# A two-layer block on one core: the mixing's weights multiplied first, and attention outputs with channels on the partitions

## The chip, the core and the metric

The kernel runs on one core of a Trainium2 chip. A core has five engines that run side by side, each with its own instruction queue that it works off in order: TensorE (PE, matrix products, results only into PSUM), VectorE (DVE), ScalarE (ACT, activation functions and scaled copies), GpSimd (POOL) and SyncE (SP), which here issues nearly all DMAs. PEld is the loading of TensorE's stationary operand. An engine waits for another through semaphores. The metric is the device time of one execution in microseconds (us), lower is better; times of several executions are given as a median.

## What is computed

The input `x` has 4 sequences of 256 tokens with 256 channels, in float32. Two layers follow, each with two residual steps: attention and a feed-forward part. Before each step, the activations are multiplied by a ratio that comes from a second input (a scan in both directions). All arithmetic is float32.

```python
x = x + L0_attn(L0_cond(x, ...), ...)     # gated delta rule, 32 value heads of 128 channels
x = x + L0_ffn(L0_cond2(x, ...), ...)     # 64 routed experts and a shared one
x = x + L1_attn(L1_cond(x, ...), ...)     # a gated mixing, see below
x = x + L1_ffn(L1_cond2(x, ...), ...)     # 8 routed experts
```

The change touches two of them. The end of the first layer's attention, where `core` are the attention outputs per head (128 channels, normalized by their own mean square), `z` are gates from the activations, and `norm_w` is a weight per channel:

```python
out = core * rsqrt(mean(core * core, -1) + EPS) * norm_w
out = out * silu(z)
return out @ w_out
```

And the second layer's mixing, with `W_in` of 1024 x 256 and `conv_w` of 512 x 512:

```python
xz = einsum('bsh,ih->bsi', hidden_states, W_in)
x, z = split(xz, 2, axis=-1)
x = einsum('bsk,ik->bsi', x, conv_w)
y = x * D
return einsum('bsi,hi->bsh', y * silu(z), W_out)
```

Nothing stands between the first half of `W_in` and `conv_w`, so the two products are one linear map of 256 channels onto 512.

## The kernel before

The 1024 tokens are worked in two halves `s` of 512 tokens (two sequences each). `x` stays in SBUF with channels on the partitions. Attention is worked in 32 units: 16 key heads by 2 halves. A unit holds one key head and its two value heads (`v`), two sequences (`b`) and two chunks of 128 tokens (`n`), so a tile of 128 x 512 holds all of one kind for a chunk. Four units form a group, for which small triangular inverses are computed together on VectorE; two units together are projected by `w_out` (`project`, L769) into one PSUM bank, and added to `x`.

In a unit, `products` (L882) makes keys, queries, norms and decay matrices; `values` (L1089) makes the values, turns them on TensorE to tokens on the partitions (`ps_vt`) and scales them on VectorE into `vo`; `outputs` (L1133) makes new values `vn0`, `vn1` and the outputs of the two chunks, `ps_at`, each copied by ScalarE into `vo`; `gates` (L1237) makes `z` with tokens on the partitions, and ScalarE's silu of it, `zs`; `normed` (L1301) makes the sums of squares with eight ScalarE activations with an accumulator (`junko`, `rs`), adds `eo` and takes the power −1/2 on GpSimd, multiplies by the roots and by `zs` on GpSimd, turns the result on TensorE (`ps_ot`, four transposes a bank) and evicts it through ScalarE, scaled by `norm_w`, into `oT` with channels on the partitions, which is what `project` needs.

After a half's attention follow `experts64` (L2013), `gated_mix` (L2114) and `experts8` (L2176). `gated_mix` makes four `xi` tiles and four `z` tiles of 128 x 512 by products that contract 256 channels (`ps_in`), then four mixing tiles that contract the 512 channels of `xi` (`ps_mix`), which VectorE multiplies by `D` and `z`, then `ps_out`.

**The order of the work** is set by a planner in the kernel, before it is built. Every step is recorded on a tape as an operation with an engine, an assumed cost, what it reads and writes, and how late its result lands (`Tape.op`, L195). `plan` (L292) places the operations one at a time: on each engine, among those that can start soon, the one whose latest allowed start is earliest. Numbers tuned for this kernel steer it: a price for a change of ScalarE's function table (`SWITCH`), for idle time (`IDLE`), for buffers taken early (`RATE`, `SPARE`), due times. `pushed` (L391) computes new latest starts from a plan; `run` (L405) repeats this `ROUNDS` times, here 10, and takes the shortest plan. The instructions are then issued in that order on each engine.

Tiles of 128 x 512 in SBUF share 59 places (`PLACES`); `MOST` (L1462) says how many each kind may hold. Six PSUM banks (`ps`) are shared in the same way. Two units of the first half (`EARLY`, heads 3 and 4) have their gates made early, in the opening, and kept in DRAM. Matmuls of float32 take two records each in the profile. All instructions are recorded through one helper, so that they have one line, L128 (L129 in the changed file); they are told apart by tile names.

Of the kernel before, what the change touches and what calls it, by code (L numbers as in the profile page):

```python
# [12 lines left out]
ALU = mybir.AluOpType  # L13
# [46 lines left out]
def _lay_out(i):  # L60
# [36 lines left out]
    d["winT"] = _rows(i["L1_attn_W_in"].T)  # L97
# [84 lines left out]
class Tape:  # L182
# [222 lines left out]
    def run(self):  # L405
# [7 lines left out]
        for o, (o.start, o.end, o.new) in zip(self.ops, min(plans)[2]):  # L413
            pass
# [6 lines left out]
ROUNDS, SWITCH, LOAD, SPARE, AHEAD, EACH, END, IDLE, MOMENT, GAP, RATE, GIVES = 10, 14.532, 1.3, 95.787, 163.973, 23.222, 1300.0, 54.829, 0.668, 62.664, 3.14, 4.877  # L421
UNIT = 42

EARLY, FEW = range(3, 5), 6
NORMS = 0.55
FOUR32, TWO64 = 0.75, 1.1
LAND = 3.0
WINDOW, ENOUGH, LITTLE, SLOW, THIN = 3.4, 0.471, 0.38, 0.5, 6.598
# [367 lines left out]
class Unit:  # L796
# [85 lines left out]
    def products(self):  # L882
# [107 lines left out]
        op("DVE", 0.78, shifted, [ps], [turned, k2, ki, self.eo])  # L990
# [98 lines left out]
    def values(self):  # L1089
# [17 lines left out]
        for n in range(2):  # L1107
# [13 lines left out]

            def scaled(n=n, ps=ps, vo=vo):
# [8 lines left out]
            op("DVE", _dve(512), scaled, [ps, self.kn], [vo])  # L1131

    def outputs(self):  # L1133
# [38 lines left out]
        def decayed():  # L1172
# [4 lines left out]
            "at0",  # L1177
            lambda q: self.attnT[0]()[:, q, :],
            lambda q: vn0()[:, q, :],
            [self.attnT[0], vn0],  # L1180
        )
        copied(lambda: vob(0), ps, vo[0])
        ps = product(
# [42 lines left out]
        ps = p.ps(f"at1_{self.tag}")  # L1226

        def second():
            for q in range(4):
                o = ps()[:, q * P : q * P + P]  # L1230
                e.tensor.matmul(o, qe()[:, q, :], vd()[:, q, :], start=True, stop=False)
                e.tensor.matmul(o, self.attnT[1]()[:, q, :], vn1()[:, q, :], start=False, stop=True)

        op("PE", 2 * cost, second, [qe, vd, self.attnT[1], vn1], [ps])
        copied(lambda: vob(1), ps, vo[1])

    def gates(self, early=False):  # L1237
# [4 lines left out]
        if self.kept:  # L1242
            for n, (kept, keptb) in enumerate(self.kept):
                zs = self.buf([P, 2, 2, P], "zs", 3, name=n)
# [11 lines left out]
        for n in range(2):  # L1256
            zs = self.buf([P, 2, 2, P], "zse" if early else "zs", 3, name=n)
            of.append(zs)
            ps = p.ps(f"z{n}_{self.tag}")

            def products(n=n, ps=ps):
                for b in range(2):
# [38 lines left out]
    def normed(self):  # L1301
# [8 lines left out]

        def o(n):
            return vo[n]().rearrange("p v b d -> p (v b) d")

        def roots(n):
            return rs()[:, n].rearrange("p v b -> p (v b)")

# [940 lines left out]
```

## Time and profile before

| | |
|---|---|
| time, median of 3 runs (lowest to highest) | 1409.51 us (1408.84 to 1413.2) |
| the profiled execution's own time | 1412.93 us |
| its span | 1411.1 us |
| its mean granted TensorE clock | 0.982 |
| ScalarE: table loads | 126, 161.7 us |
| ScalarE: squares `junko`, and reading the accumulator | 79.3 us and 47.8 us |
| ScalarE: `oT` from `ps_ot`, `vo` from `ps_at` | 40.4 us and 36.8 us |
| GpSimd: `vo` by the roots, `vo` by `zs`, the power | 66.8, 81.2 and 54.6 us |
| VectorE: `vo` from `ps_vt` | 42.1 us |
| VectorE: `turned` from `ps_kt` | 32 times, 14.2 us |
| DMA queue of SP | 35.5% of the 16 engines' time, 143.45 MB |

In the profile, a group line reads: line, engine, operation, out<-in by tile names, shapes, count | busy time, mean duration of one in ns | idle time of the engine just before these instructions and what ended it. Busy time is the union of the instructions' durations, and matmuls overlap, so busy time divided by the count is the spacing and the mean is the whole duration. A line of stages gives the stretch, its length, then the busy time of each engine with its number of instructions, the granted clock, the share of the DMA engines and their rate. A DMA line gives the tile, count, size and the median time from issue to landing.

### The profile page before, as it was taken

What the parts mean: (1) busy time and instruction counts of PE and PEld (TensorE: products, weight loads), DVE (VectorE), ACT (ScalarE), POOL (GpSimd) and SP (SyncE); (2) the same over time, 40 slices, a digit from 0 to 9 for tenths busy, and PEclk for the clock granted to TensorE, in tenths of its full rate; (3) what the DMA queues carried; (4) which work ended last, traced back from release to release, by engine and by line L of the source; (5) the groups of instructions that cost most, each with busy time, mean ns of one, the idle gap of its engine ahead of it and who ended that gap; (6) DMA issues with size and microseconds to landing.
All of it is one profiled execution on the core that took longest, in us unless ns stands there. A gap on an engine that the chain in (4) does not pass through costs nothing.

```text
span 1411.1 us, 24205 instructions
## 1 busy us (share of the span) xinstructions
PE 1321.2 (94%) x8428; PEld 817.4 (58%) x8428; DVE 1064.8 (75%) x2112; ACT 915.2 (65%) x1999; POOL 922.8 (65%) x913
## 2 busy tenths in 40 slices
PE   5986999999999899999999999999999999998988
PEld 3544766765875676766676576555455544443433
DVE  7889798787699588768769879867796787773123
ACT  1797799999889899988898898533434622211220
POOL 3189769979763988976885884487654666762032
PEclk9997999999999999999999999999999999999989
DMA  6412524412322353241351343544532324656030
GB/s 208 129 46 64 128 83 113 125 62 67 91 90 58 71 140 106 50 139 39 94 139 38 76 124 101 150 127 135 153 105 83 103 92 139 181 139 212 0 105 15
DMA packets 149817, 145.39 MB, mean 103 GB/s; under 512 B 76976, under 2 KB 93104, under 8 KB 149696
## 3 DMA queue, kind: packets, MB, share of 16 engines
q1 hardware_dynamic: 149264, 143.45, 35.5%
q8 instruction: 67, 1.10, 0.3%
q14 instruction: 54, 0.44, 0.1%
q10 hardware_dynamic: 432, 0.40, 0.1%
HBM read 129.75 MB, written 14.06 MB: 102 GB/s over the span
## 4 chain that ended last, share of the span: by engine, by line
PE 45%; DVE 25%; ACT 12%; POOL 7%; DMA 6%; issue 5%; SPq 1%; ACTq 0%; POOLq 0%; DVEq 0%
PE ps_h L128 5%; PE ps_a L128 4%; PE ps_ae L128 4%; PE ps_wo L128 4%; PE ps_e L128 4%; PE ps_z L128 4%; DVE xs L128 3%; DVE prod L128 3%; DVE accv_v L128 3%; PE ps_cvv L128 3%; PE ps_at L128 2%; DVE accq_q L128 2%; POOL attnT L128 2%; DMA w_w<-in_w 2%; ACT L128 2%
## 5 line engine op out<-in xcount | busy, mean ns | idle before, releaser
L128 ACT ACT_TABLE_LOAD x126 | 161.7, 1283 | 22.2 <-DVE sb_xT L128 10.4
L128 DVE SCALAR_TENSOR_TENSOR accv_v<-ps_cvv,sb_convw,accv_v 128x510 f32<-128x510 f32 (+2 forms) x192 | 141.8, 744 | 42.3 <-ACT accv_v L128 37.4
L128 PE MATMUL ps_z<-wz,ratio 128*128 128x256 f32 x480 | 118.7, 394 | 9.6 <-DVE vo L128 6.6
L128 POOL TENSOR_TENSOR hw_h<-hw_h,r_h 128x512 f32<-128x512 f32 x64 | 85.7, 1347 | 63.9 <-DVE hw_h L128 63.3
L128 PE MATMUL ps_h<-ratio,w_w 128*128 128x512 f32 x256 | 118.9, 598 | 6.6 <-DMA w_w<-in_w 5.7
L128 PE MATMUL ps_cvv<-ratio,wv 128*128 128x512 f32 x256 | 119.9, 601 | 2.9 <-ACT kqm L128 1.0
L128 ACT ACTIVATE r_h<-ps_h 128x512 f32<-128x512 f32 x64 | 38.2, 596 | 126.8 <-PE ps_h L128 126.5
L128 PE MATMUL ps_a<-hw_h,w_w 128*128 128x512 f32 x256 | 118.2, 593 | 0.0
L128 PE MATMUL ps_wo<-oT,wo 128*128 128x512 f32 x256 | 113.0, 593 | 0.0
L128 POOL TENSOR_TENSOR hw_e<-hw_e,r_e 128x512 f32<-128x512 f32 x32 | 41.6, 1322 | 101.0 <-DVE hw_e L128 101.0
L128 PEld LDWEIGHTS ps_z<-wz,ratio 128*128 128x128 f32 x480 | 90.1, 196 | 24.6 <-DVE vo L128 6.8
L128 PEld LDWEIGHTS ps_h<-ratio,w_w 128*128 128x128 f32 x256 | 47.0, 190 | 70.2 <-issue 55.1
L128 DVE TENSOR_TENSOR xs<-xs,prod 128x30 f32<-128x30 f32 (+14 forms) x240 | 81.2, 338 | 8.2
L128 DVE TENSOR_TENSOR prod<-xs,Rt 128x30 f32<-128x30 f32 (+14 forms) x240 | 78.5, 327 | 11.6 <-ACT xs L128 5.9
L128 ACT ACTIVATE junko<-vo 128x128 f32<-128x128 f32 x256 | 79.3, 310 | 7.6
L128 PE MATMUL ps_at<-vn,attnT 128*128 128x128 f32 x512 | 82.3, 277 | 1.5 <-ACT vn L128 1.4
L128 POOL TENSOR_TENSOR X<-attnT,kqm 128x512 f32<-128x512 f32 x64 | 82.8, 1313 | 1.2 <-ACT kqm L128 1.0
L128 POOL TENSOR_TENSOR vo<-vo,zs 128x512 f32<-128x512 f32 x64 | 81.2, 1288 | 1.6 <-ACT zs L128 1.6
L128 PEld LDWEIGHTS ps_wo<-oT,wo 128*128 128x128 f32 x256 | 48.1, 190 | 57.4 <-issue 52.6
L128 POOL TENSOR_TENSOR attnT<-attnT,sb_consts 128x512 f32<-128x512 f32 x56 | 70.7, 1280 | 15.5 <-DMA attnT<-G 8.5
L128 POOL TENSOR_TENSOR attnT<-attnT,kqm 128x512 f32<-128x512 f32 x64 | 80.6, 1278 | 0.1
L128 PEld LDWEIGHTS ps_a<-hw_h,w_w 128*128 128x128 f32 x256 | 47.9, 190 | 56.2 <-issue 52.6
(253 smaller groups left out, 3412.5 us busy)
## 6 DMA issues: line engine op xcount, KB each, us to landing
attnT<-G SPq DMA_DIRECT2D x64, 256.0 KB, 5.2
w_w<-in_w SPq DMA_DIRECT2D x64, 256.0 KB, 4.4
wb_wb<-w_rows SPq DMA_DIRECT2D x128, 128.0 KB, 3.6
wqk<-in_wqk SPq DMA_DIRECT2D x32, 256.0 KB, 4.2
wv<-in_wv SPq DMA_DIRECT2D x32, 256.0 KB, 4.2
wo<-in_wo SPq DMA_DIRECT2D x32, 256.0 KB, 3.8
qe<-G SPq DMA_DIRECT2D x32, 256.0 KB, 4.5
wz<-in_wz SPq DMA_DIRECT2D x30, 256.0 KB, 4.6
```

The source lines that it names most:

```text
L128: return self._tc.keep_in_program_order(f(*a, **k))
```

## The change

It has three parts and new numbers for the planner.

1. *The mixing's two weights are multiplied first* (`joined`, new). The first half of `W_in` and `conv_w` are loaded in six loads at the start, multiplied by eight matmuls of 512 columns into two tiles, copied by ScalarE and written to DRAM. `gated_mix` no longer makes `xi`; it loads the two product tiles and contracts the 256 channels of the activations with them.
2. *Attention outputs with channels on the partitions.* The operands of the output products are swapped, and `z` is made with its weight as the stationary operand (512 columns at once), so both come out with channels on the partitions and stay in PSUM or need no turning: no copy into `vo`, no `ps_ot`. The two chunks' outputs are made together, after both new values. ScalarE squares whole banks; TensorE sums the squares over the partitions with a matrix of ones (`ps_on`, eight matmuls, as for the keys); VectorE turns the sums and adds `eo`; GpSimd takes the power. The roots, with tokens on the partitions, are written to DRAM as rows (`rs`, 1024 values) and read back spread over all partitions (`rb`, two DMAs). VectorE multiplies the outputs by `norm_w` and `zs` into `oT`, and GpSimd multiplies `oT` by `rb`.
3. *The values are scaled by ScalarE*, in two halves, in place of one VectorE instruction.

The planner takes the last of 2 rounds' plans in place of the shortest of 10, has other prices, limits and due times, and a third unit's gates (head 5) are made early.

```diff
-        for o, (o.start, o.end, o.new) in zip(self.ops, min(plans)[2]):
+        for o, (o.start, o.end, o.new) in zip(self.ops, plans[-1][2]):
...
-ROUNDS, SWITCH, LOAD, SPARE, AHEAD, EACH, END, IDLE, MOMENT, GAP, RATE, GIVES = 10, 14.532, 1.3, 95.787, 163.973, 23.222, 1300.0, 54.829, 0.668, 62.664, 3.14, 4.877
-UNIT = 42
-EARLY, FEW = range(3, 5), 6
+ROUNDS, SWITCH, LOAD, SPARE, AHEAD, EACH, END, IDLE, MOMENT, GAP, RATE, GIVES = 2, 11.958, 1.3, 87.21, 174.585, 24.024, 1286.888, 56.776, 0.687, 66.3, 3.538, 5.035
+UNIT = 42.358
+EARLY, FEW = range(3, 6), 5
...
+            def evicted(n=n, ps=ps, vo=vo):
+                for b in range(2):
+                    e.scalar.activation(
+                        vo()[:, :, b, :],
+                        ps().rearrange("p (v b d) -> p v b d", v=2, b=2)[:, :, b, :],
+                        AF.Copy,
+                        scale=self.kn()[:, 2 * n + b : 2 * n + b + 1],
+                    )
...
-        copied(lambda: vob(0), ps, vo[0])
...
+        for v in range(2):
+            ps = p.ps(f"at{v}_{self.tag}")
+            self.out.append(ps)
+            def heads(v=v, ps=ps):
+                for b in range(2):
+                    q = 2 * v + b
+                    for n in range(2):
+                        o = ps()[:, (2 * b + n) * P : (2 * b + n) * P + P]
+                        last, vn = self.attnT[n]()[:, q, :], (vn0, vn1)[n]()[:, q, :]
+                        if n:
+                            e.tensor.matmul(o, vd()[:, q, :], qe()[:, q, :], start=True, stop=False)
+                        e.tensor.matmul(o, vn, last, start=not n, stop=True)
...
+                    e.tensor.matmul(ps(), wz()[:, k, v * P : v * P + P], p.act[s][:, k, :], start=k == 0, stop=k == 1)
...
+        op("PE", NORMS, norms, sqs, [sums], to=[turned, rs])
+        op("DVE", 0.66, shifted, [sums, self.eo], [turned, rs])
+        op("POOL", 1.64, lambda: tt(rs(), rs(), p.neghalf, ALU.pow), [], [rs])
+            lambda: e.sync.dma_start(out=rows.rearrange("x t -> t x"), in_=rs()),
...
+                lambda ps=ps, zs=zs, oT=oT: v_.scalar_tensor_tensor(oT(), ps(), p.normw, zs(), ALU.mult, ALU.mult),
...
+                row = rows.rearrange("(v x) t -> v (x t)", v=2)[v : v + 1]
+                e.sync.dma_start(out=rb(), in_=row.to_broadcast([P, 512]))
+            op("POOL", 1.28, lambda rb=rb, oT=oT: tt(oT(), oT(), rb(), ALU.mult), [rb], [oT])
...
+    def joined(self):
+        winx = [load(f"winx{i}", t["winx"][:, 2 * i : 2 * i + 2], 2) for i in range(2)]
+        mixT = [load(f"mixT{k}", t["mixT"][:, k : k + 1], 1) for k in range(4)]
+        for c in range(2):
+                for k in range(4):
+                    at = k % 2 * C + c * P
+                    lhsT = winx[k // 2]()[:, at : at + P]
+                    e.tensor.matmul(ps(), lhsT, mixT[k](), start=k == 0, stop=k == 3)
...
-        for two in range(4):
+        for two in range(2):
...
+        for c, (kept, keptb) in enumerate(p.mix):
+            op("SP", 0.45, lambda w=w, kept=kept: e.sync.dma_start(out=w(), in_=kept), [keptb], [w], late=3.5)
...
-                4,
-                lambda k, w=w: w()[:, k * P : k * P + P],
-                lambda k: xi[k](),
+                2,
+                lambda k, m=m: mix[k]()[:, m * P : m * P + P],
+                lambda k: act()[:, k, :],
```

## The prediction

> **What bounds the kernel now.** I read the page's busy table first, then the busy time by stage (opening, attention of half 0, attention of half 1 beside the first expert layers, the rest), then the groups by shape, the timeline of the mixing, and the DMA issues.
>
> ```profile
> PE 1321.2 (94%) x8428; PEld 817.4 (58%) x8428; DVE 1064.8 (75%) x2112; ACT 915.2 (65%) x1999; POOL 922.8 (65%) x913
> core 0: us, PE busy (x) PEld busy (x) DVE busy (x) ACT busy (x) POOL busy (x), PEclk, DMA share, GB/s
> 0.00:141.00 141.00, 100.78 (x421) 64.41 (x422) 120.64 (x262) 91.06 (x175) 85.23 (x87) 0.89 0.36 112
> 141.00:700.00 559.00, 535.82 (x4704) 376.10 (x4704) 453.16 (x932) 499.36 (x1145) 433.64 (x432) 0.99 0.34 92
> 700.00:1110.00 410.00, 401.81 (x2624) 250.71 (x2624) 324.98 (x622) 259.06 (x571) 272.94 (x275) 1.00 0.40 111
> 1110.00:1300.00 190.00, 184.71 (x457) 82.42 (x457) 134.04 (x242) 43.36 (x78) 111.13 (x106) 1.00 0.50 150
> 1300.00:1411.00 111.00, 98.08 (x230) 43.74 (x228) 31.93 (x56) 22.33 (x34) 19.89 (x16) 0.94 0.11 38
> ```
>
> TensorE idles 40.2 us in the opening, 23.2 + 8.2 us from 141 to 1110, 5.3 + 12.9 us behind that. So outside the opening a TensorE microsecond taken away is nearly a microsecond of the span.
>
> ```profile
> L128 PE MATMUL ps_ot<-sb_consts,vo 128*128 128x128 f32 x256 | 35.0, 276 | 3.7 <-DVE acck_k L128 2.1 <-POOL vo L128 1.4
> L128 PE MATMUL ps_kt<-sq,ones 128*32 128x128 f32 x512 | 21.7, 288 | 10.6 <-ACT kqm L128 7.1 <-DVE accv_v L128 1.4 <-DVE acck_k L128 1.3
> L128 PE MATMUL ps_in<-ratio,w_win 128*128 128x512 f32 x64 | 28.2, 594 | 1.8 <-DVE ratio L128 1.8
> L128 PE MATMUL ps_mix<-hw_xi,w_mix 128*128 128x512 f32 x64 | 27.8, 592 | 0.0
> L128 PE MATMUL ps_z<-wz,ratio 128*128 128x256 f32 x480 | 118.7, 394 | 9.6 <-DVE vo L128 6.6 <-DVE accq_q L128 1.4 <-issue 1.0
> L128 PE MATMUL ps_cvv<-ratio,wv 128*128 128x512 f32 x256 | 119.9, 601 | 2.9 <-ACT kqm L128 1.0 <-ACT vo L128 0.8 <-DVE accv_v L128 0.7
> L128 ACT ACTIVATE junko<-vo 128x128 f32<-128x128 f32 x256 | 79.3, 310 | 7.6
> L128 DVE SCALAR_TENSOR_TENSOR wb_z<-ps_mix,sb_dskip,wb_z 128x512 f32<-128x512 f32 x4 | 3.0, 751 | 25.5 <-ACT wb_z L128 13.6 <-PE ps_mix L128 11.9
> ```
>
> Busy time is a union, so busy by count is the spacing of the two records that make one matmul; the mean of one is its whole duration.
>
> ```profile
> 1066.70 13.90 PE L128 MATMUL ps_mix<-hw_xi,w_mix 128*128 128x512 f32 x32
> 31.27 3.85 PE L128 MATMUL ps_gates<-sb_wba,ratio 128*128 128x64 f32 x16 [7.12 <-DVE ratio L128]
> 34.91 3.73 PE L128 MATMUL ps_cvq<-ratio,wqk 128*128 128x512 f32 x4
> 40.66 1.88 PE L128 MATMUL ps_cvq<-ratio,wqk 128*128 128x512 f32 x4
> raw<-X SPq DMA_DIRECT2D x32, 128.0 KB, 3.2
> attnT<-G SPq DMA_DIRECT2D x64, 256.0 KB, 5.2
> ```
>
> The mixing runs back to back; the first gates and `cvq` after an idle 7 us take twice what the next `cvq` takes; the last two rows are the nearest to the new trips through DRAM.
>
> The trace-reading page disagrees with the first reading. The Trainium skill, "Perfetto Trace Analysis", Identifying the Most-Contended Engine, says that matmul busy time misleads and that weight-load busy time tells the headroom; that is 58% here, below VectorE's 75%, so by it VectorE would bind and its added 28 us (below) would give 1441. The back-to-back mixing row decides against it.
>
> **TensorE's part.** All from the groups above.
> - Input and mixing: the four `xi` products go (28.2 / 2 = 14.1) and the mixing contracts 256 instead of 512 (27.8 / 2 = 13.9): −28.0. Half of it stands alone near the end, half between full work.
> - Transposes of the output: −35.0.
> - Sums of squares by the ones matrix: the same eight matmuls as the keys' norms, `ps_kt`: +21.7.
> - Gates `z`: 16 matmuls of 256 columns become 8 of 512 per unit. 118.7 + 7.8 (the two early units) against 256 records at the `ps_cvv` spacing (119.9 / 256 = 0.468), 119.9: −6.6; bounds −6.6 and 0, as steady spacing is 0.43 per 512 and 0.215 per 256. I take −6.6, since rows of whole groups are compared.
> - A third unit's `z` goes early: 119.9 / 32 = 3.7 moves into the opening, whose idle 40.2 us covers it: −3.7; bounds −3.7 and 0.
> - The product of the two weights: eight 512-column matmuls, 16 × 0.44 = 7.0, stand among the `ratio` sums before the gates. TensorE is idle there from about 24 to 31.27: 0. Cover gone (loads late), it costs 7, or 14 at half clock. Its six loads go out behind the first `wqk`; by 12 us 2.9 MB has moved, by 20 us over 5 MB, and the first product stands where the sums were at 21.4 us.
> - It also keeps TensorE busy until the gates: 3.85 + 3.73 could fall by 1.8 each (the other half's gates: 5.9 − 3.85 = 2.05). Between −4 and +3 (the second product delays the gates): −3.
>
> The attention products keep their count (12 of 128 columns a unit).
>
> **The other engines** (cover: TensorE). ScalarE loses the squares (79.3 and 47.8 of accumulator reads), the copies of `ps_at` (36.8) and `oT` (40.4), the `xi` copies (4.8); it gains 64 squares at about 0.60, 128 halves of `vo` at about 0.42 (between 0.376 for a 256-column scaling out of PSUM and 0.412), and 25 more table loads (151 instead of 126 in the changed program's instruction order, which is known before it runs) at 1.283: 209 off, 126 on, −83. GpSimd: −7.6 − 66.8 − 81.2 + 64 × 1.28 = −74. VectorE: −42.1 + 64 × 0.751 + 32 × 0.443 + 32 × about 0.25 = +28. The one that waits less is ScalarE, at 499 of 559 us in half 0; the one that waits more is VectorE, at 453. Its new transposition waits for TensorE's sums (17.0 us in all for the same instruction on `ps_kt`), and the convolution's taps and the triangular inverse stand behind it. TensorE's 31.4 us of waits between 141 and 1110 could shrink by half or grow by VectorE's 28: 0, since gain and loss meet different engines. The planner's changed numbers lie within these bounds.
>
> SP issues about 100 more DMAs and blocks for each root (up to 3.2 us, 32 times), with the loads of `wqk`, `wo`, `attnT`, `qe` behind it. SP already waits 162 us for GpSimd's `fwn` alone while TensorE waits 5.7 us for weights: 0.
>
> **The new trip before `wo`.** Sums → transposition and shift 0.69 (0.443 and 0.25) → root 1.65 (the median of `rs` by `neghalf`) → row written 3.2 → two spreads, 5.2 and 0.45 for the second's issue → last product 1.28 (`vo` by `zs`), and some 0.5 from engine to engine: 13.0 us. In the changed order I laid TensorE's rows at their steady spacing and took the work between a pair's last sums and its `wo`: 11.9, 15.6, 14.3, 14.1, 14.7, 20.7, 14.8, 13.4, 14.3, 12.6, 13.6, 14.9, 14.0, 13.5, 21.5, and 5.9 for the last pair. The last one falls short by 7.1, and the `e` products queue behind it: +7 (0 if VectorE or ScalarE is later anyway). The other fifteen miss 1.5, or 14 if queues add 2 us each: +5, nearer the trip without queues.
>
> No row shows a write of 4-byte pieces. Its 1024 pieces equal those of `raw` (32 × 32 runs of 128 bytes), 3.2; below it the gates' row, 1.5 for 128 runs; above, 6.8, the longest of that family. I take 3.2.
>
> The Trainium skill, "DMA: Bandwidth & Descriptors", Rules for kernel authors, speaks against this write: a non-contiguous last dimension gives a descriptor per element, and it says to rearrange. Its Specifications add a read-modify-write under 512 B. Doubling the landing to 6.4 for that is my estimate; the sum by it would be 27 us higher, 1394.
>
> **Sum.** −28.0 − 35.0 + 21.7 − 6.6 − 3.7 − 3 + 7 + 5 = −42.6. The profiled execution took 1412.93 (span 1411.1), 3.4 above the median 1409.51 of the runs shown: 1370.3 in its terms, 1367 as a median.
>
> **Rivals** (as medians).
> - *VectorE takes the attention's gain*: its 28 us all come on the path, 1395. For: 81% in half 0 and in-order waits. Against: ScalarE, now the fullest there, gets lighter.
> - *Relief*: half of TensorE's 31.4 us go because ScalarE and GpSimd shed 83 and 74: 1351. Against: few of its waits name them.
> - *The weights' loads come late*: 14 at half clock and the warm 3 lost, 1384. Against: the bytes above.
> - *The root comes late* (slower): if the write lands x later, the sixteen shortfalls add up; at x = 4.3 (7.5 us) they eat the gain of 54.6 that stands without them, and at x = 8 they are 106.6, giving 1461. For: no row has so small a piece. Against: `raw` never took over 6.8.
>
> **Chances.** As forecast 0.60; relief 0.14; VectorE 0.12; late loads 0.04; late root 0.10, of which 0.02 lands near no change. Under 0.3% (4 us) a measurement of this kernel tells nothing. Faster 0.90, same 0.02, slower 0.08. The low end is relief with the last pair's wait hidden, 1351 − 7 − 4 = 1340; the high end passes VectorE's case, 1400.
>
> **What would show it.** Right: TensorE busy near 1280; no `ps_ot`; `ps_mix` at half; VectorE's busy up some 28, ScalarE's and GpSimd's down some 80; TensorE's waits before `wo` under 15 us in all. Wrong: `ps_wo` waiting for GpSimd's `oT` several us in every pair, the row's write landing beyond 7 us, or TensorE's waits from 141 to 700 well over 23 us with VectorE as their cause.

## The result and the profile after

| | before | after |
|---|---|---|
| time, median | 1409.17 us (1407.52 to 1413.2) | 1576.97 us (1568.57 to 1577.7) |
| ratio | | 1.1174, 95% interval 1.1153 to 1.1195 |
| profiled execution, span | 1411.1 us | 1566.7 us |
| TensorE idle in the span | 89.9 us | 220.0 us |
| mean granted clock | 0.982 | 0.937 |

The change costs 168 us where a gain of 42 was predicted. From the page of the changed kernel, the busy times and the chain of work that ended last (its shares by engine, then by line):

```profile
PE 1346.7 (86%) x8380; PEld 762.2 (49%) x8380; DVE 1099.4 (70%) x2176; ACT 860.2 (55%) x1570; POOL 844.3 (54%) x817
...
PEclk9989888998999999898899999989999969999999
...
PE 40%; DMA 23%; DVE 16%; POOL 8%; ACT 7%; issue 5%; SPq 2%; POOLq 0%; ACTq 0%; DVEq 0%
DMA rs<-rs 8%; DMA rb<-rs 6%; PE ps_wo L129 6%; PE ps_h L129 5%; PE ps_a L129 5%; PE ps_e L129 4%; PE ps_ae L129 4%; PE ps_cvv L129 2%; DMA done<-Rt_c 2%; DVE xs L129 2%; DMA w_w<-in_w 2%; POOL oT L129 2%; DVE prod L129 2%; PE ps_z L129 2%;
```

The same line of the kernel before:

```profile
PE 45%; DVE 25%; ACT 12%; POOL 7%; DMA 6%; issue 5%; SPq 1%; ACTq 0%; POOLq 0%; DVEq 0%
```

In the chain of before, DMA had 6%; here it has 23%, and 8% are the writes of the root rows, `rs<-rs`, which the prediction took as short. The stretches of the prediction's own table, in the changed kernel:

```profile
0.00:141.00 141.00, 109.19 (x404) 61.25 (x405) 119.37 (x245) 94.42 (x179) 75.80 (x81) 0.92 0.40 127
141.00:700.00 559.00, 476.45 (x4092) 301.72 (x4091) 411.36 (x842) 387.98 (x744) 342.35 (x329) 0.93 0.42 96
700.00:1110.00 410.00, 347.56 (x2488) 201.40 (x2487) 291.10 (x620) 238.60 (x429) 217.29 (x204) 0.93 0.45 103
```

In the opening TensorE is busy 8.4 us longer than before, of which 7.2 are the new product of the two weights; so hardly more of the old work is done there, and the first gates start later than before (31.27 us in the prediction's lines):

```profile
22.29 3.60 PE L129 MATMUL ps_mix<-mix_mixT,mix_winx 128*128 128x512 f32 x8
...
34.64 3.76 PE L129 MATMUL ps_gates<-sb_wba,ratio 128*128 128x64 f32 x16 [2.73 <-DVE ratio L129]
38.19 3.39 PE L129 MATMUL ps_cvq<-ratio,wqk 128*128 128x512 f32 x4
```

From there on every engine is emptier and the clock granted is 0.93, so no engine is the bound; all wait. What for, in the waits of SP's queue, of GpSimd and of TensorE (total us, times, longest):

```profile
SPq L129 <- DMA rs<-rs: 225.7, 29, 11.1
```
```profile
POOL oT L129 <- DMA rb<-rs: 197.6, 31, 14.5
...
POOL attnT L129 <- DMA attnT<-G: 63.7, 7, 12.3
```
```profile
PE ps_wo L129 <- POOL oT L129: 82.5, 17, 12.7
PE ps_ks L129 <- POOL vd L129: 20.8, 6, 9.3
```

This is one path: the write of the roots, the spread, GpSimd's product, and then TensorE before `wo`, in nearly every pair. Pieces of the chain from 180 to 420 us (start, length, what) show how long each takes:

```profile
187.64 14.08 DMA attnT<-G
...
248.64 10.63 DMA rs<-rs
259.35 3.20 DMA rb<-rs
...
348.77 10.81 DMA rs<-rs
```

A write of 4 KB takes over 10 us. `attnT`, a load with nothing to do with the roots, takes 14.08 us here (the median of its kind was 5.2 before); it stood behind such a write on SP's queue. Between 188 and 197 us the DMA engines are busy for 19% of the time and move 6 GB/s, so it is not bytes that they are short of:

```profile
188.00:197.00 9.00, 8.70 (x74) 6.39 (x73) 7.55 (x23) 8.42 (x18) 1.60 (x2) 1.00 0.19 6
```

The groups by shape, busy and mean ns of one; the first line is from the kernel before:

```profile
L128 PE MATMUL ps_wo<-oT,wo 128*128 128x512 f32 x256 | 113.0, 593 | 0.0
...
L129 PE MATMUL ps_wo<-oT,wo 128*128 128x512 f32 x256 | 145.2, 718 | 82.6 <-POOL oT L129 82.5
L129 PE MATMUL ps_z<-ratio,wz 128*128 128x512 f32 x232 | 115.6, 626 | 2.1 <-ACT U L129 1.2 <-DVE accq_q L129 0.8
L129 PE MATMUL ps_on<-sqo,ones 128*32 128x128 f32 x512 | 23.2, 281 | 6.7 <-ACT sqo L129 5.6 <-issue 1.0
L129 PE MATMUL ps_in<-ratio,w_win 128*128 128x512 f32 x32 | 14.6, 599 | 1.8 <-DVE ratio L129 1.8
L129 PE MATMUL ps_mix<-ratio,w_mix 128*128 128x512 f32 x32 | 14.1, 592 | 0.0
...
L129 PE MATMUL ps_mix<-mix_mixT,mix_winx 128*128 128x512 f32 x16 | 7.2, 592 | 0.0
```

The work changed as counted: no `ps_ot`, the mixing at half. But `wo`, untouched by the change, went from 113.0 us to 145.2: it stands right behind the wait and runs at a colder clock (718 ns for one, 593 before). Behind one such wait, of 11.2 us until 381.9, the granted clock was 0.50 from 382 to 385 us and 0.89 from 385 to 389.

### The profile page after: what moved, and what is told of

Same layout as the page of the kernel before. It is cut to its first block, busy times and chain, and to the rows that moved or that the text cites. A ratio compares the mean times of both kernels' runs of the same rounds, so it can differ in the third digit from the quotient of the medians.

```text
span 1566.7 us, 23865 instructions
## 1 busy us (share of the span) xinstructions
PE 1346.7 (86%) x8380; PEld 762.2 (49%) x8380; DVE 1099.4 (70%) x2176; ACT 860.2 (55%) x1570; POOL 844.3 (54%) x817
## 2 busy tenths in 40 slices
DMA packets 189303, 163.33 MB, mean 104 GB/s; under 512 B 111344, under 2 KB 122352, under 8 KB 189184
## 4 chain that ended last, share of the span: by engine, by line
PE 40%; DMA 23%; DVE 16%; POOL 8%; ACT 7%; issue 5%; SPq 2%; POOLq 0%; ACTq 0%; DVEq 0%
DMA rs<-rs 8%; DMA rb<-rs 6%; PE ps_wo L129 6%; PE ps_h L129 5%; PE ps_a L129 5%; PE ps_e L129 4%; PE ps_ae L129 4%; PE ps_cvv L129 2%; DMA done<-Rt_c 2%; DVE xs L129 2%; DMA w_w<-in_w 2%; POOL oT L129 2%; DVE prod L129 2%; PE ps_z L129 2%; DMA attnT<-G 2%
## 5 line engine op out<-in xcount | busy, mean ns | idle before, releaser
L129 PE MATMUL ps_wo<-oT,wo 128*128 128x512 f32 x256 | 145.2, 718 | 82.6 <-POOL oT L129 82.5
L129 POOL TENSOR_TENSOR oT<-oT,rb 128x512 f32<-128x512 f32 x64 | 81.0, 1280 | 197.8 <-DMA rb<-rs 197.6
L129 PEld LDWEIGHTS ps_wo<-oT,wo 128*128 128x128 f32 x256 | 56.8, 232 | 164.4 <-POOL oT L129 105.8
L129 PE MATMUL ps_cvv<-ratio,wv 128*128 128x512 f32 x256 | 125.6, 622 | 5.5 <-ACT acck_k L129 3.6
L129 PE MATMUL ps_z<-ratio,wz 128*128 128x512 f32 x232 | 115.6, 626 | 2.1 <-ACT U L129 1.2
L129 DVE TENSOR_TENSOR sb_xT<-sb_xT,ps_wo 128x512 f32<-128x512 f32 x32 | 21.8, 682 | 100.4 <-PE ps_wo L129 100.3
L129 PE MATMUL ps_at<-attnT,vn 128*128 128x128 f32 x512 | 84.3, 277 | 3.8 <-ACT vn L129 3.1
L129 DVE SCALAR_TENSOR_TENSOR hw_h<-ps_h,wb_wb 128x512 f32<-128x512 f32 x64 | 43.7, 683 | 61.7 <-ACT r_h L129 42.6
L129 ACT ACTIVATE attnT<-attnT,nG 128x128 f32<-128x128 f32 x224 | 70.1, 391 | 19.0 <-POOL attnT L129 18.7
```

Source lines behind the costliest of these rows:

```text
L129: return self._tc.keep_in_program_order(f(*a, **k))
```

## The experiments

### What the small pieces cost

**The same bytes in fewer pieces.** The order of all engines is kept; only the address pattern of the row's write is another, and the roots land permuted.

```diff
-            lambda: e.sync.dma_start(out=rows.rearrange("x t -> t x"), in_=rs()),
+            lambda: e.sync.dma_start(
+                out=rows.rearrange("x t -> (x t)").rearrange("(t x) -> t x", x=8), in_=rs()),
```

> The changed kernel with one address pattern altered: the row of roots is written as 128 contiguous pieces of 32 bytes instead of 1024 pieces of 4 bytes. The order of every engine's instructions, the wait of the spreads for the write and the bytes moved stay. The roots land in the row in another order, so the rows spread are permuted and the output is not the reference's. Theory P (the 4-byte pieces make the write land late, and all else follows): the spreads' wait for the write falls from 8.6 to 12.7 us per unit to about 2 (a gates' row of 128 runs took 1.5), GpSimd's waits for the spread rows from 197.6 us to under 40, and the time to 1365 to 1405. Rival B (SP blocks in order at every root whatever the piece, and the loads behind it come late): the waits stay over 5 us each and the time stays above 1500. Rival C (TensorE's lower clock or VectorE takes the gain): the write is quick, GpSimd's waits go, and the time still stays above 1430.

Measured: 1411.26 us, 1.0018 of before (0.9994 to 1.0041). From the DMA issues (median us to landing, last) and GpSimd's waits:

```profile
rs<-rs SPq DMA_DIRECT2D x32, 4.0 KB, 1.4
```
```profile
POOL oT L129 <- DMA rb<-rs: 30.8, 16, 6.6
```

With 128 pieces of 32 bytes the write lands in 1.4 us, and 166 of the 168 us are gone. The pages count 189303 DMA packets for the changed kernel and 160631 here: 28672 fewer, which is 32 times 1024 − 128, so the pieces are what was altered. That is theory P in its mechanism, but not in its figure: the time stays 6 us above the range that was given, and 44 above the prediction. So there are two errors to find, and the pieces are one of them.

**Without the wait for the write.**

```diff
-                row = rows.rearrange("(v x) t -> v (x t)", v=2)[v : v + 1]
-                e.sync.dma_start(out=rb(), in_=row.to_broadcast([P, 512]))
+                e.sync.dma_start(
+                    out=rb().rearrange("p (x t) -> p x t", t=P),
+                    in_=p.G[self.s][v : v + 1, 4 * self.h : 4 * self.h + 4, :].to_broadcast([P, 4, P]))
```

> The changed kernel with its order, but the two spreads read a row of the solved matrices in DRAM, long finished, instead of the row of roots; the write of 4-byte pieces is still made and nobody waits for it. The output is not the reference's, since the factors are others. Theory P (the latency of the write is what costs): GpSimd's waits for the spread rows fall under 60 us, and the time to 1365 to 1420. Rival Q (the 4-byte pieces themselves, 32768 of them, hold up the other transfers on the queue): a load of the output matrices issued behind such a write still lands 10 us or more after its issue, and the time stays over 1450. Rival C (clock, VectorE): over 1430 without any wait on a spread row.

Measured: 1567.23 us (1562.6 to 1571.87), 1.1088 (1.0991 to 1.1186). GpSimd's waits:

```profile
POOL oT L129 <- DMA rb<-G: 179.0, 34, 14.1
POOL attnT L129 <- DMA attnT<-G: 74.0, 13, 12.2
```

Rival Q holds. The spreads need nothing of the write: the first go out 1.1 us behind it instead of 9.9. They still come late, and so does the load of `attnT` that was issued at 187.7, half a microsecond behind the write: GpSimd waits for it until 201.9. The spreads' own reading pattern is another here, but the page counts the same 189303 packets. So the 1024 pieces hold up what is issued behind them on the queue.

**The write from another queue.**

```diff
-            lambda: e.sync.dma_start(out=rows.rearrange("x t -> t x"), in_=rs()),
+            lambda: e.scalar.dma_start(out=rows.rearrange("x t -> t x"), in_=rs()),
```

> The changed kernel with its 4-byte pieces, but the write is issued from ScalarE's DMA queue instead of SP's; the spreads still wait for it, on SP. Theory R (the pieces hold up only the transfers that stand behind them on their own queue): the spreads and loads on SP's queue land in their usual 3 to 5 us, only the write's own latency is left, and the time is 1420 to 1480. Rival S (the pieces hold up all 16 DMA engines, whatever the queue): loads issued at the same time are as late as before, and the time is 1530 to 1590.

Measured: 1556.76 us, 1.1046 (1.1024 to 1.1068). The issues, and the waits of SP's queue and of GpSimd:

```profile
attnT<-G SPq DMA_DIRECT2D x64, 256.0 KB, 5.6
rb<-rs SPq DMA_DIRECT2D x64, 256.0 KB, 5.1
w_w<-in_w SPq DMA_DIRECT2D x64, 256.0 KB, 4.3
...
rs<-rs ACTq DMA_DIRECT2D x32, 4.0 KB, 10.6
```
```profile
SPq L129 <- DMA rs<-rs: 304.1, 28, 30.6
```
```profile
POOL oT L129 <- DMA rb<-rs: 207.0, 30, 17.5
```

Neither theory had this whole. R was right that the pieces hold up only their own queue: the loads on SP's queue land in 4.3 to 5.6 us again. Its time was wrong by 77 us, because SP now stands 304 us in all waiting for the writes, and what GpSimd needs comes as late as before. So either harm is enough alone: the pieces on SP's queue (without a wait, 1567), or their own 10.6 us with a wait (1557). Against the 32-byte pieces, 145.5 us come from 9.2 us more of landing: 15.8 us of time for each, about one for each of the 16 pairs. On the way to 10.6 us hardly a pair has any slack left.

The Trainium skill, "DMA: Bandwidth & Descriptors", Queues, rings and completion order, says that an engine of the DMA takes turns between the queues that have work for it and takes the descriptors of each ring in order. The 14.08 us behind a write on the same queue and the 5.6 us beside a write on another agree with it.

**Four roots to a piece, output whole.** The row is kept as two times 128 tokens by four roots, 256 pieces of 16 bytes, and GpSimd reads the spread factors with a stride of four.

```diff
-        rows, rowsb = p.dram.tile([8, P], F32, name=name, tag=name), p.stays(name)
+        rows, rowsb = p.dram.tile([2, P, 4], F32, name=name, tag=name), p.stays(name)
...
-            lambda: e.sync.dma_start(out=rows.rearrange("x t -> t x"), in_=rs()),
+                out=rows.rearrange("v t x -> t v x"), in_=rs().rearrange("p (v x) -> p v x", v=2)
...
+                o = oT().rearrange("p (x t) -> p x t", t=P)
+                tt(o, o, rb().rearrange("p (t x) -> p x t", x=4), ALU.mult)
```

> The changed kernel with its output whole, but the roots kept four to a token: the row is written as 256 pieces of 16 bytes instead of 1024 of 4, and GpSimd reads the spread factors with a stride of four. No instruction is added and the order stays. Theory (the number and size of the pieces set everything that the change lost beyond the kernel before): 1405 to 1420, the write landing in 1.4 to 3 us. Rival (256 pieces still hold up the queue): a write of over 4 us and 1430 or more. Rival (strided reading slows GpSimd): its product goes from 1.29 to over 1.6 us, and the time by 64 x 0.3 = 20 us at most.

Measured: 1416.77 us, 1.0054 (1.0036 to 1.0072). The write lands in 2.7 us. GpSimd's product by the spread roots:

```profile
L129 POOL TENSOR_TENSOR oT<-oT,rb 128x512 f32<-128x512 f32 x64 | 98.4, 1557 | 41.6 <-DMA rb<-rs 41.4
```

It takes 1557 ns instead of 1280 in the changed kernel, 17.4 us more in all. The later landing and the slower product together cost 5.5 us by the medians, so near 1.4 us a little is still hidden. The change is now whole and does what it says, and it is 0.5% slower than the kernel before.

Two other ways out were not measured: an order of the engines laid out for a landing of 9.5 us (the planner reckons with 3.0), and roots turned on TensorE first, so that the row is 8 pieces of 512 bytes. How much of the 168 us an order made for the late landing would have hidden stays open.

### Why the rest does not gain

With small pieces gone, TensorE's terms came in nearly as priced (in the run with 32-byte pieces: `ps_ot` −35.0, input −13.6, mixing −13.7, the product of the weights +7.2, `ps_on` +22.9, `z` −3.5: −35.7 in all, where the prediction's terms for the same groups give −40.9), but TensorE's busy time fell only by 9.8, to 1311.4 where near 1280 was to show the prediction right. The other products grew by 26 in all. The mean granted clock was 0.973 instead of 0.982; by itself that is 0.9%, an estimate of 10 of the 26, and the rest isn't explained. TensorE's idle time rose from 89.9 to 100.6. So I took work away from one engine at a time, in the kernel before and with its order kept.

**TensorE, in the mixing.**

```diff
-            for k in range(k_n):
-                p.e.tensor.matmul(ps(), lhsT(k), rhs(k), start=k == 0, stop=k == k_n - 1)
+            half = name in ("in0", "in1", "in2", "in3", "mix0", "mix1", "mix2", "mix3")
+            last = (k_n // 2 if half else k_n) - 1
+            for k in range(last + 1):
+                p.e.tensor.matmul(ps(), lhsT(k), rhs(k), start=k == 0, stop=k == last)
```

> The kernel before with its order kept, and only TensorE work taken away in the mixing: the four xi products contract one of two blocks, the mixing two of four, so the mixing's result is not the reference's. It takes 16 records of ps_in and 32 of ps_mix away, 7.0 + 13.9 = 20.9 us of TensorE. Theory T (TensorE's time there is on the path, whatever the order): 1386 to 1392. Rival K (half 0's share, about 10, covers the last pair's chain; only half 1's share arrives): 1396 to 1402. Rival N (nothing arrives): 1406 to 1413.

Measured: 1399.85 us, 0.9923 (0.9895 to 0.9951): 10 of 21 us arrive. One stretch of the kernel before, then two of this one:

```profile
900.00:1110.00 210.00, 208.26 (x934) 113.40 (x933) 157.49 (x234) 92.75 (x193) 134.92 (x138) 1.00 0.43 123
...
900.00:1110.00 210.00, 201.22 (x919) 110.43 (x918) 158.42 (x237) 93.65 (x196) 135.53 (x139) 0.99 0.42 123
1110.00:1300.00 190.00, 184.57 (x451) 81.53 (x449) 134.13 (x241) 43.48 (x76) 109.97 (x105) 1.00 0.48 150
```

Rival K. In the kernel before, TensorE was busy 208.3 us from 900 to 1110, where half 0's mixing stands; here 201.2, and it does the same from 1110 to 1300 (184.6 against 184.7). So half 0's share became idle time, and half 1's share, behind which little else is left, came off the end: from 1300 us to the end, 111 us before, 98 are left, with 12.6 us less of TensorE.

**TensorE, in the attention.**

```diff
-                    for k in range(2):
+                    for k in range(1):
                         e.tensor.matmul(
                             ps()[:, b * 256 : b * 256 + 256],
...
-                            stop=k == 1,
+                            stop=True,
```

> The kernel before with its order kept, and only TensorE work taken away in the attention: the gates z contract one of two blocks (the output is not the reference's). Half of 118.7 + 7.8 = 63.2 us of TensorE goes, spread evenly over the 32 units. It prices a TensorE microsecond in the attention, which the prediction took at nearly one. Theory T: 1347 to 1360. Rival W (waits for VectorE and ScalarE, and the clock that falls behind each wait, take a good part): 1370 to 1395.

Measured: 1412.67 us, 1.0015 (0.9995 to 1.0035). From the page, and half 0's attention:

```profile
PE 1289.4 (91%) x8172; PEld 778.4 (55%) x8172; DVE 1069.8 (76%) x2112; ACT 914.5 (65%) x1999; POOL 922.7 (65%) x913
```
```profile
141.00:700.00 559.00, 519.13 (x4529) 356.04 (x4520) 457.54 (x927) 497.81 (x1140) 430.69 (x430) 0.97 0.34 92
```

Nothing arrives, which neither theory had. `z` fell by 54 us (118.7 to 68.0 and 7.8 to 4.3), the busy time only by 32, at a clock of 0.971 instead of 0.982, and TensorE's idle time grew by 32. VectorE, ScalarE and GpSimd do in these 559 us what they did before, within 5 us. **TensorE was 96% busy in this stretch, and less work for it did not shorten the run.** Only `z` was tried; that other products of the attention are off the path too is not shown.

**The other engines.** More VectorE work; less ScalarE, VectorE and GpSimd work, each alone; and less of three at once.

VectorE scales each tile of values twice:

```diff
                 e.vector.tensor_tensor(
                     vo(),
                     ps().rearrange("p (v b d) -> p v b d", v=2, b=2),
                     norms.to_broadcast([P, 2, 2, P]),
                     ALU.mult,
                 )
+                e.vector.tensor_tensor(
+                    vo(),
+                    ps().rearrange("p (v b d) -> p v b d", v=2, b=2),
+                    norms.to_broadcast([P, 2, 2, P]),
+                    ALU.mult,
+                )
```

> The kernel before with its order kept, in which VectorE scales each tile of values twice (the same result written twice): 64 x 0.682 = 43.6 us more for VectorE, two thirds of it beside the attention of half 0, nothing else. It prices VectorE's added work, which the prediction took at nothing. Theory T (TensorE covers it): 1410 to 1420. Rival V (VectorE's in-order chain holds TensorE up): 1430 to 1455.

ScalarE's squares on 4 columns instead of 512:

```diff
-                for q in range(4):
-                    e.scalar.activation(
-                        junk(), o(n)[:, q, :], AF.Square, accum_out=roots(n)[:, q : q + 1]
-                    )
+                e.scalar.activation(junk()[:, :4], o(n)[:, :, 0], AF.Square)
+                e.scalar.copy(roots(n), junk()[:, :4])
```

> The kernel before with its order kept, in which ScalarE's squares of the outputs and their accumulator reads are replaced by two instructions of 4 columns (the output is not the reference's): some 79.3 + 47.8 - 25 = 100 us less for ScalarE. Theory S (ScalarE, busy 499 of 559 us in the attention of half 0, sets the pace there): 1340 to 1395. Rival (it is covered): 1404 to 1414.

One tap of the values' convolution left out:

```diff
-            for d in (1, 2, 3):
+            for d in (1, 2) if name[0] == "v" else (1, 2, 3):
```

> The kernel before with its order kept and one of the three taps of the values' convolution left out (the output is not the reference's): 47.8 us less for VectorE, as much as e12_dve added. Theory V2 (VectorE binds in both directions): 1365 to 1385. Theory V1 (all engines are packed alike: work added to VectorE costs, work taken from one engine alone gives little): 1398 to 1410.

GpSimd's product by the roots on 4 columns:

```diff
-                lambda n=n: tt(o(n), o(n), _over(roots(n), 2, P), ALU.mult),
+                lambda n=n: tt(rs()[:, n], rs()[:, n], rs()[:, n], ALU.mult),
```

> The kernel before with its order kept, in which GpSimd's 64 products of output and root (66.8 us) are replaced by 64 products of 4 columns (the output is not the reference's), some 60 us less for GpSimd. Theory G (GpSimd, the slowest to finish its part of a unit, sets the pace): 1355 to 1390. Rival (covered like the others): 1402 to 1412.

The edits of e10_zhalf, e13_act and e14_tap together:

> The kernel before with its order kept and the three reliefs of e10_zhalf, e13_act and e14_tap together: some 63 us less for TensorE, 100 for ScalarE, 48 for VectorE (the output is not the reference's). Alone they gave 0, 0 and -5. Theory A (these engines are packed alike, and each alone is held by the others): 1340 to 1375. Rival L (the pace of the attention is set by what none of them does: GpSimd, the trips through DRAM, the buffers): 1390 to 1407.

| edit of the kernel before | busy time of that engine | time | ratio |
|---|---|---|---|
| e12_dve, VectorE more | 1064.8 to 1112.3 | 1443.87 us | 1.0245 (1.0214 to 1.0277) |
| e13_act, ScalarE less | 915.2 to 843.9 | 1410.8 us | 1.001 (0.9999 to 1.0022) |
| e14_tap, VectorE less | 1064.8 to 1023.2 | 1404.37 us | 0.9954 (0.9935 to 0.9972) |
| e19_pool, GpSimd less | 922.8 to 866.3 | 1409.96 us | 0.9999 (0.9979 to 1.0019) |
| e18_three, TensorE, ScalarE and VectorE less | 41, 72 and 40 us less | 1401.44 us | 0.993 (0.9907 to 0.9953) |

VectorE is priced on one side only: 47.5 us more of it cost 34, and 41.6 less gave 5. ScalarE and GpSimd give nothing. Three at once give 9, so it is not that these three are merely packed alike (theory A): most of the pace is set by something that taking these instructions away does not touch. The chain of work of the kernel with three engines relieved:

```profile
PE 49%; DVE 29%; ACT 8%; DMA 4%; POOL 4%; issue 4%; SPq 1%; ACTq 0%; DVEq 0%; POOLq 0%
```

It still goes through all engines (TensorE 49%, 45% in the kernel before). From 141 to 700 us it has 1102 pieces, half a microsecond each in the mean, that go from engine to engine. What it is that cannot be shortened there, the latency from engine to engine in the fixed order, the trips through DRAM or buffers that come free late, these runs don't tell; relieving all four engines together was not tried.

**The change with VectorE's addition taken off.** In the whole-output form with 16-byte pieces, order kept, the same tap is left out as in e14_tap.

```diff
-            for d in (1, 2, 3):
+            for d in (1, 2) if name[0] == "v" else (1, 2, 3):
```

> e6_rows with its order kept and the same tap left out: VectorE's work falls by 47.8 us, to the amount that the kernel before had, while TensorE keeps the change's savings. Theory V (VectorE's added 49 us are what eats the gain): 1370 to 1388. Rival C (waits and clock of the new order, whatever VectorE does): 1405 to 1417.

Measured: 1413.18 us (1404.54 to 1419.38), 1.0016 (0.9993 to 1.004), VectorE busy 1065.6 instead of 1113.7. By the medians it is 3.6 us below the same kernel with all taps, as e14_tap was 5.4 below the kernel before; its runs spread over 15 us. So the amount of VectorE's added work is not what eats the gain: theory V falls. Whether the place of the added instructions, between the outputs and `wo`, costs something is not tested by it.

**VectorE's addition given to ScalarE and GpSimd**, with other planner numbers:

```diff
-                "DVE",
-                lambda ps=ps, zs=zs, oT=oT: v_.scalar_tensor_tensor(oT(), ps(), p.normw, zs(), ALU.mult, ALU.mult),
+                "ACT",
+                lambda oT=oT, ps=ps: e.scalar.activation(oT(), ps(), AF.Copy, scale=p.normw),
...
+            op("POOL", 1.28, lambda zs=zs, oT=oT: tt(oT(), oT(), zs(), ALU.mult), [zs], [oT])
```

> e6_rows with the 64 products of output, weight and gate taken from VectorE: ScalarE scales the output out of PSUM (64 x 0.69 = 44 us), GpSimd multiplies by the gate (64 x 1.28 = 82 us); VectorE loses 48. Seven planner numbers are others. Output whole. Theory V: 1370 to 1395. Rival (GpSimd's longer chain before wo comes on the path): 1405 to 1425.

Measured: 1416.23 us (1403.48 to 1421.6), 1.0068 (1.0048 to 1.0087). VectorE's busy time fell to 1076.8 and nothing came of it. That fits the run before it, but it is weak by itself: its order is another too (ScalarE loads 122 tables instead of 151), and the next runs show what an order alone can do.

### The parts alone, and other orders of the same work

**The mixing alone**, in the kernel before, planner numbers of before:

```diff
-    d["winT"] = _rows(i["L1_attn_W_in"].T)
+    d["winT"] = _rows(i["L1_attn_W_in"][512:].T)
+    d["winx"] = _rows(i["L1_attn_W_in"][:512])
...
+            self.joined()
...
-                4,
-                lambda k, w=w: w()[:, k * P : k * P + P],
-                lambda k: xi[k](),
+                2,
+                lambda k, m=m: mix[k]()[:, m * P : m * P + P],
+                lambda k: act()[:, k, :],
```

> The kernel before with the mixing part of the change alone (the two weights multiplied first, four input products and half the mixing gone), under the planner numbers of before; attention untouched. The prediction's own terms: input and mixing -28.0, warm clock at the gates -3, product of the weights 0: 1378 to 1385. Rival D (the stretches that lose TensorE work are held by VectorE's sums or by loads there, so part of the 28 comes back as waits): 1388 to 1402. Rival E (the opening pays for the two products and six loads): 1400 to 1415.

Measured: 1420.11 us, 1.0077 (1.0057 to 1.0097), above every range that was given. It takes 10 us off TensorE's busy time (1311.2), the product of the weights included, and it is slower. One wait of TensorE between 1080 and 1160 us stands out, which the kernel before does not have:

```profile
PE ps_ot L129 <- POOL vo L129: 13.1, 3, 11.9
```

The last pair's transposes now wait for GpSimd. In the kernel before, 5.3 us of `z` and 1.9 of `ps_lg` stand between the last attention outputs and these transposes, and 7.0 of `ps_e` among them; here the planner has left only 1.9 us of `z` there. ScalarE loads 133 tables instead of 126, and the clock was 0.97.

**The attention part alone**, with 16-byte pieces and the changed kernel's planner numbers; against e6_rows the lines of the last diff are undone:

```diff
-            self.joined()
...
-        for two in range(2):
+        for two in range(4):
...
-                2,
-                lambda k, m=m: mix[k]()[:, m * P : m * P + P],
-                lambda k: act()[:, k, :],
+                4,
+                lambda k, w=w: w()[:, k * P : k * P + P],
+                lambda k: xi[k](),
```

> The attention part of the change alone, in the whole-output form with 16-byte pieces, and the mixing of before; the planner numbers are the changed kernel's. The prediction's terms for this part are -35.0 + 21.7 - 6.6 - 3.7 + 7 + 5 = -11.6: 1396 to 1400. If the parts add up by what the runs gave (6 us more than before for both parts with 16-byte pieces, 10 more for the mixing alone): 1403 to 1408. Rival (VectorE's added work comes on the path): 1415 to 1430.

Measured: 1437.43 us, 1.0209 (1.0162 to 1.0255), again above every range. With the mixing part alone at +11 and this at +28, both together are at +7: the parts don't add up, since the planner lays out another order each time, with numbers chosen for one of them. So I changed the planner's numbers and nothing else.

Against e6_rows:

```diff
-SWITCH, SPARE, MOMENT, GIVES, THIN = 11.958, 87.21, 0.687, 5.035, 11.607
+SWITCH, SPARE, MOMENT, GIVES, THIN = 15.052, 79.214, 0.689, 6.209, 15.636
```

> e6_rows with six of the planner's numbers altered (the weights of table loads, spare places, thin stretches), which lays out another order of the same work. It asks how much of the missing gain is the luck of one order. Theory L (the missing 40 us are the order's): 1370 to 1395. Rival M (the missing gain is in waits and clock dips that any such order has): within 10 us of e6_rows.

Against e6_rows:

```diff
-ROUNDS, SWITCH, SPARE, MOMENT, GIVES, ENOUGH = 2, 11.958, 87.21, 0.687, 5.035, 0.436
+ROUNDS, SWITCH, SPARE, MOMENT, GIVES, ENOUGH = 3, 11.51, 108.835, 0.696, 4.921, 0.386
```

> e6_rows in a third order (other planner numbers than e6_rows and e8_replanned). Orders of the same work gave 1417 and 1403. Theory O (the time of this kernel is its order's as much as its work's): anywhere from 1390 to 1430. Rival (the order matters little): within 4 us of 1410.

Against e5_mixing:

```diff
-SWITCH, SPARE, IDLE, MOMENT, GIVES, ENOUGH = 14.532, 95.787, 54.829, 0.668, 4.877, 0.471
+SWITCH, SPARE, IDLE, MOMENT, GIVES, ENOUGH = 17.593, 93.608, 52.276, 0.585, 4.186, 0.629
```

> e5_mixing (the mixing part alone) with six planner numbers altered: another order of the same work. Theory O (the 10 us that e5 lost are its order's, and the part itself gains at least what e9_mixhalf gained, 10): 1385 to 1403. Rival (the part itself costs): 1412 to 1425.

| the same work, other orders | time | ratio |
|---|---|---|
| whole change, 16-byte pieces (e6_rows) | 1416.77 us | 1.0054 (1.0036 to 1.0072) |
| whole change, e8_replanned | 1403.48 us | 0.9961 (0.994 to 0.9982) |
| whole change, e21_rowsplan | 1426.07 us | 1.0105 (1.0064 to 1.0146) |
| mixing alone, e5_mixing | 1420.11 us | 1.0077 (1.0057 to 1.0097) |
| mixing alone, e20_mixplan | 1396.34 us | 0.9893 (0.9853 to 0.9933) |

Orders of the same work lie 23 and 24 us apart, which is as much as most terms of the prediction's sum. Of these, e8_replanned fell between its two theories: 13 us below e6_rows, where the rival had 10 at most, and 8 above the range of the theory that the missing gain is the order's. The mixing part in the order of e20_mixplan is the best kernel of the study, 1.1% faster than before. Its stretch in half 0's attention, to be read beside that of before in the prediction:

```profile
141.00:700.00 559.00, 537.58 (x4729) 379.98 (x4729) 471.37 (x958) 478.39 (x1129) 443.14 (x441) 0.98 0.33 93
```

It does 25 more TensorE records and more of VectorE's and GpSimd's work in the same time, with 114 table loads on ScalarE instead of 126. How much of its gain is the mixing's and how much the order's is open: the kernel before was not tried in other orders.

## Why the prediction was wrong

- *"So outside the opening a TensorE microsecond taken away is nearly a microsecond of the span."* Wrong, and the sum rests on it. 54 us of `z` taken from the attention gave nothing; of 21 from the mixing, 10. The row that decided for it, half 0's mixing back to back, is the very share that became idle time in e9_mixhalf. The busy share says how full an engine is, not that it sets the pace; the page's chain, of which TensorE was 45%, was the view to read, and I did not use it. The chain still promised more than it gave: `ps_z` was 4% of it.
- *"No row shows a write of 4-byte pieces ... I take 3.2."* Wrong: 10.6 us. The row of `raw` had as many pieces, but of 128 bytes; 128 pieces of 32 bytes took 1.4 and 256 of 16 took 2.7. The rule that I weighed, a descriptor per element and a penalty below 512 B, pointed the right way; the doubling that I made of it, 6.4, was still too short by 4.
- *"SP ... 0."* Wrong: SP stood 225.7 us waiting for these writes, and what was issued behind one landed late. Without any wait the time was 1567.
- *The root comes late.* This rival, at 0.10, is what happened. By its formula the landing of 10.6 (x = 7.4) gives shortfalls of 98 us and 1453; measured was 1577. Of the missing 124, by one way of splitting it, 51 are the gain that did not arrive anyway (the formula has 1360 for the 32-byte pieces, measured 1411), 53 are slack that the pairs had less of than the formula reckons (the formula rises by 93 from 1.4 to 10.6, measured 146 with the write on its own queue), and 20 are the loads held up on SP's queue (1577 against 1557).
- *Input and mixing −28.0.* The busy time came as −27.3; half 0's half of it did not arrive with the order kept, and nothing did when the planner laid out a new order with the old numbers (+11). "Half of it stands alone near the end" was right.
- *VectorE +28.* The count was right: 47.1 + 14.0 + 9.2 − 42.1 = 28.2, but VectorE's busy time rose by 34.6, and by 48.9 with 16-byte pieces, since other instructions became longer (the scans `fwd`, for one, from 913 to 969 and 993 ns). Taken at nothing on the path; 47.5 us added to the kernel before cost 34, so this was no safe zero, but taking as much out of the fixed change gave back only 3.6. VectorE as the engine that takes the gain (0.12) is not confirmed. The Trainium skill, "Perfetto Trace Analysis", Identifying the Most-Contended Engine, does not trust TensorE's matmul busy time, and neither do these runs; but the engine with the highest share that it leads to, VectorE, gave 5 us for 42 taken off it, so here the share named no engine whose relief pays.
- *`z` −6.6.* It gave between +0.8 (in the changed kernel) and −3.5 (32-byte pieces). The upper bound, 0, was the nearer.
- *Product of the weights 0, warm gates −3.* Wrong, by 5 to 6 us at that place. The idle time before the gates fell from 7.1 to 2.7 us, but the first product stands before the last six `ratio` sums and moves them back from 21.40 to 25.72, so the gates start at 34.64 instead of 31.27 (33.71 with 32-byte pieces). They are hardly warmer: gates and first `cvq` together take 0.4 us less, not 3.6.
- *GpSimd −74* came as −78.5. *ScalarE −83* (its gains add up to 124, not 126) came as −55, with the 151 table loads as counted; the 47.8 us of accumulator reads lie in part inside the squares' own time, since in e13_act the groups lost 101 us and ScalarE's busy time only 71. Neither mattered for the time.
- *The range* could not hold the result: the chance of 0.10 for late roots was left outside it at full price, with a bound (6.8) taken from rows of larger pieces.

## What to carry to other kernels

Count the contiguous runs of a DMA and look at their size, not at the bytes: a few KB in 4-byte pieces cost 10 us, and all that stands behind them on the queue pays too. Where a planner has packed the engines, a busy share of 95% does not mean that the engine's work is on the path: take some of it away with the order kept before pricing a change by it, because what is freed may only become a wait. And a change of the work changes the order: with differences between orders of 23 us, compare the best of several orders on each side before a part that should save 20 us is judged.

## What the hardware showed that was not expected

- The write's landing by pieces of 4, 16 and 32 bytes: 10.6, 2.7 and 1.4 us for the same 4 KB (1024, 256 and 128 pieces). From 256 to 1024 pieces it grows about as their number; but 1024 pieces of 128 bytes (`raw`) had taken 3.2, so number alone does not explain it.
- Such a write on ScalarE's queue leaves SP's loads at 4.3 to 5.6 us; on SP's queue a load behind it took 14.08.
- With half of `z` gone the granted clock was 0.971 instead of 0.982, and only 32 of 54 us left TensorE's busy time: what was freed became waits, and `z` itself went from 394 to 415 ns. Behind a wait of 11.2 us in the changed kernel, the clock was 0.50 for the next 3 us.
- GpSimd's product of 128 x 512 took 1557 ns with one operand read at a stride of four words, 1280 without.
